# Two chained attention layers on one core: the second layer's denominators by 32x32 transposes and one product, a third buffer for its high parts, and projections one step later

## The chip, the core and the metric

The kernel runs on one core of a Trainium2 chip. The metric is the device time of one execution in microseconds, lower is better. Three executions of the kernel before are given by their median, and one more execution was profiled.

The engines have these names throughout: PE multiplies matrices (PEld is its weight load), DVE is the vector engine, ACT the scalar engine that computes exponentials, POOL the general one that here also issues many transfers, and SP only issues transfers. SBUF is the working memory of 128 partitions, and PSUM holds the results of PE.

## The reference

The input x has 4 images of 64x64 pixels with 256 channels, so 4 images of 4096 tokens. Two attention layers follow each other, each over all the tokens of one image, with queries and keys of 32 channels. The second layer has values of 128 channels and a projection back to 256.

```python
# layer 0
q, k, v = x @ Wq + bq, x @ Wk + bk, x @ Wv + bv          # 32, 32, 256 channels
attn = softmax(einsum('bnd,bmd->bnm', q, k))
x = gamma * einsum('bnm,bmc->bnc', attn, v) + x
# layer 1
f, g, v = x @ Wf + bf, x @ Wg + bg, x @ Wh + bh          # 32, 32, 128 channels
beta = softmax(einsum('bqd,bkd->bqk', g, f))
out = x + (beta @ v) @ Wo + bo
```

All arrays are in float32.

## The kernel before

`fast_path` does all the work. It computes exp of the scores without first taking off a maximum, and at its end counts on DVE and PE whether denominators, values and gamma stayed in a safe span; the count goes to a flag, and `general_path`, a slower way, would run only if the flag were above zero.

**Blocks and steps.** For each image b and layer l the queries are cut into blocks j, and the keys of a block into steps i. In the first layer (l = 0) there are 16 blocks of 256 queries, with 8 steps of 512 keys. In the second layer (l = 1) there are 8 blocks of 512 queries, with 16 steps of 256 keys. A `Step` computes the scores on PE into PSUM (`st`, L532), ACT takes exp of them into an SBUF tile `p` of 128x1024 (L544), and PE multiplies with the values and accumulates over the steps of the block (L582 in the first layer, L600 in the second).

**Parts.** A full float32 product is slow on PE, so the first layer, and six of the sixteen steps of the second (`SPLIT1`: 0, 3, 5, 8, 11, 13), are computed in parts in the faster format float32r: ACT computes exp twice, once rounded into `high` (L542) and once into `p`; DVE makes `low` = p - high (L555) and `d` from both (L560); PE makes one product from each of the three. The ten other steps of the second layer use p as a whole, in float32.

**Denominators.** In the first layer a column of ones beside the values gives the sum of the weights with the product. In the second layer it is summed apart. The p tiles of the steps in `MOVED_SUMS` (0, 4, 7, 9, 12) are summed by transfers: POOL issues a copy of the first into the tile `p_sum_moved` (L548) and adds each of the others to it with an accumulating transfer (L550). The p tiles of the eleven other steps are added by DVE into the tile `p_sum` (L571, L573). At the end of a block `end_second` adds both (L659) and folds the two halves into `sums`, 128x512 (L660). The sum over the 128 partitions is then made by PE for each 128 queries: `sums` is the loaded side and one column of ones is multiplied with it (L668), beside the output projection (L667) into the same PSUM tile. DVE takes the reciprocal (L670), ACT scales with it (L673), and POOL issues the accumulating transfer to the output (L675). There are four such outputs to a block, and `plan` puts them at steps 1 to 4 of the next block, so that those of an image's last block fall into the first layer of the next image.

**The next projections.** `project_units` makes queries, keys and values of half a block of 256 tokens in three units: a transpose of loaded squares on DVE (L392) with a split into parts, the queries and keys (L422, L439 to L446), and the values (L464). In the second layer, `plan` places those of the next image with `i = 12 + 7 * h - j * NI[1]`, h from 0 to 15: a transpose there, the queries and keys two steps later, the values three steps later. The last image has none.

**Buffers.** `wide` gives out the tiles of 128x1024. Tag "t" has two buffers, for `high` of both layers and for p of split steps in the second layer; "p" has three; "d" and "e" have one each. "d" serves `d` in the first layer and `p_sum` in the second, and "e" is for `p_sum_moved`. Tag "small" has four buffers of 128x256: for the residual rows x_res, the rows x1 of the first layer's result, and the outputs y. The projected queries and keys `qk` (L439, L440) have a buffer of their own. PSUM results beside scores and products share two buffers, `side_psum`.

**What sets the order.** The loop at the end of `fast_path` runs the steps one after the other and calls `scores()` two steps ahead. The program goes through a scheduler that keeps dependencies, allots the buffers and orders each engine's instructions by its own estimate; each engine then runs its instructions strictly in that order. An instruction that waits stops all that stands behind it on its engine.

Of the kernel before, what the change touches and what calls it, by code (L numbers as in the profile page):

```python
# [57 lines left out]
P = 128  # L58
# [10 lines left out]
MOVED_SUMS = (0, 4, 7, 9, 12)  # L69
# [169 lines left out]
def fast_path(ctx: ExitStack, tc: tile.TileContext, x, w0, w1, wo, bo, gamma, out, off):  # L239
# [27 lines left out]
    def wide(tag, name, dtype=F32):  # L267
        return work.tile([P, 2 * QB], dtype, tag=tag, bufs={"d": 1, "e": 1, "p": 3}.get(tag, 2), name=name)
# [41 lines left out]

    inverse = const.tile([P, 2, B * N // P], F32, name="inverse")
# [12 lines left out]
    for l, (q_w, q_b, k_w, k_b, v_w, v_b) in enumerate((w0, w1)):  # L324
        queue = (nc.scalar, nc.gpsimd)[l]
        w_sb = work.tile([P, NCC, 2 * D], F32, tag="small", bufs=4, name=f"wqk_whole{l}")
        b_sb = const.tile([2 * D, 1], F32, name=f"bqk{l}")
        for g, w_dram, b_dram in ((0, q_w, q_b), (D, k_w, k_b)):
            queue.dma_start(w_sb[:, :, g : g + D], w_dram.rearrange("(c p) d -> p c d", p=P))
            queue.dma_start(b_sb[g : g + D, :], b_dram.rearrange("(d o) -> d o", o=1))  # L330
        w_parts = const.tile([P, NCC, 4 * D], F32R, name=f"wqk{l}")
        high, low = w_parts[:, :, : 2 * D], w_parts[:, :, 2 * D :]
        nc.scalar.copy(high, w_sb)
        nc.vector.tensor_sub(low, w_sb, high.bitcast(F32))
        wqk.append(w_parts)
        bqk.append(b_sb)
        v_sb = const.tile([P, NCC, CV[l]], F32, name=f"wv{l}")
        queue.dma_start(v_sb, v_w.rearrange("(c p) d -> p c d", p=P))
        wv.append(v_sb)
# [20 lines left out]
    def bias_units():  # L360


        def issue():
            nc.vector.tensor_scalar(bv, bv, gamma_sb, None, ALU.mult)
            wide_bias = work.tile([P, P], F32, tag="small", bufs=4, name="wide_bias")
# [10 lines left out]
    q_t, moved_sums, first_p, waiting = {}, {}, [], {}  # L376
# [35 lines left out]
    def project_units(b, l, h):  # L412
# [5 lines left out]
        def qk_unit():  # L418
# [10 lines left out]
            whole = data.tile([2 * D, QB0], F32, tag="qk", name=f"qk_{b}_{l}_{h}")  # L429
# [61 lines left out]
    def load_rows(dst, parts, which, order):  # L491
        for n, h in enumerate(order):
            nc.gpsimd.dma_start(dst[n * D : (n + 1) * D, :], parts[h, which])
# [16 lines left out]
    def small(name):  # L510
        return work.tile([P, C], F32, tag="small", bufs=4, name=name)


    class Step:
# [8 lines left out]
        def scores(self):  # L523
# [16 lines left out]
            if self.split:  # L540
                self.high = wide("t", f"high_{self.key}", F32R)
                nc.scalar.activation(self.high, s_flat, AF.Exp, bias=down)  # L542
            self.p = wide("t" if self.split and l == 1 else "p", f"p_{self.key}")
            nc.scalar.activation(self.p, s_flat, AF.Exp)  # L544
            if l == 1 and i in MOVED_SUMS:
                if i == MOVED_SUMS[0]:
                    moved_sums[b, j] = wide("e", f"p_sum_moved_{b}_{j}")
                    nc.gpsimd.dma_start(moved_sums[b, j], self.p)  # L548
                else:
# [14 lines left out]
        def add_up(self, p_sum):  # L564
# [5 lines left out]
            elif self.i == kept[1]:  # L570
                nc.vector.tensor_add(p_sum, first_p.pop(0), self.p)  # L571
            else:
                nc.vector.tensor_add(p_sum, p_sum, self.p)  # L573
# [80 lines left out]
    def end_second(b, j, acc, p_sum, o):  # L654
        key = f"{b}_{j}"
        for h in range(QB // QB0):
            nc.vector.tensor_add(o[h][:, :QB0], o[h][:, :QB0], acc[1][:, h * QB0 : (h + 1) * QB0])
        sums = work.tile([P, QB], F32, tag="sums", bufs=1, name=f"sums_{key}")
        nc.vector.tensor_add(p_sum, p_sum, moved_sums[b, j])  # L659
        nc.vector.tensor_add(sums, p_sum[:, :QB], p_sum[:, QB:])  # L660

        def output(t):
            def issue():
# [4 lines left out]
                nc.tensor.matmul(ps[:, C : C + 1], sums[:, tok], ones[:, :1], start=True, stop=True)  # L668
                n = (b * N + j * QB) // P + t
                nc.vector.reciprocal(inverse[:, 1, n : n + 1], ps[:, C : C + 1])  # L670
# [8 lines left out]
        return [output(t) for t in range(NT)]  # L679

    def run(units):
        for u in units:
            u()

# [15 lines left out]
    acc, p_sum, units = None, None, {}  # L700

    def plan(b, l, j, ends):
# [20 lines left out]
        else:  # L723
            for n, u in enumerate(ends):
                put(1 + n, u)
        if b + 1 < B:
            for h in range(NH):
                i = 12 + 7 * h - j * NI[1]
# [6 lines left out]
    for n, s in enumerate(steps):  # L735
        b, l, j = s.b, s.l, s.j
        if s.first:
# [5 lines left out]
            if l == 1:  # L743
                p_sum = wide("d", f"p_sum_{b}_{j}")
# [24 lines left out]
        s.add_up(p_sum)  # L769
# [31 lines left out]
        if s.last:  # L801
            ends = end_first(b, j, acc) if l == 0 else end_second(b, j, acc, p_sum, o)
    run(ends)

    good = small("good").rearrange("p (l n) -> p l n", l=2)
    nc.vector.tensor_scalar(good, inverse, 1.0 / SUM_MAX, None, ALU.is_ge)
    nc.vector.tensor_scalar(inverse, inverse, 1.0 / SUM_MIN, None, ALU.is_le)
    nc.vector.tensor_mul(good, good, inverse)  # L810
    nc.vector.tensor_scalar(seen_v, seen_v, VALUE_MAX, None, ALU.is_le)
    size = const.tile([P, 1], F32, name="size")
    nc.vector.tensor_mul(size, gamma_sb, gamma_sb)
    nc.vector.tensor_scalar(size, size, GAMMA_MAX**2, None, ALU.is_le)
    low = const.tile([P, 1], F32, name="low")
    for seen, axes in ((good, AX.XY), (seen_v, AX.XY)):
        nc.vector.tensor_reduce(low, seen, axes, ALU.min)
        nc.vector.tensor_mul(size, size, low)
# [54 lines left out]
```

## Time and profile before

| what | value |
|---|---|
| median of three executions | 3158.18 us (3157.30 to 3159.27) |
| the profiled execution: own time | 3155.92 us |
| the profiled execution: span from first to last instruction | 3154.1 us, 1.8 us less |
| PE, PEld busy | 3116.3 us (99%), 2672.0 us (85%) |
| DVE busy | 2689.1 us (85%) |
| ACT busy | 2140.1 us (68%) |
| POOL busy | 900.7 us (29%) |
| transfers | 239.49 MB, mean 76 GB/s |
| granted clock of PE, mean | 0.998 |

A row of a group in the profile names line, engine and operation, output and inputs, shapes and count; behind the first bar stand busy time and mean duration of one, behind the second how long the engine had been idle just before, and for whom. A row of the timeline has its start in us, its length, the engine, and how many equal instructions follow each other. Matmuls overlap, so their modelled lengths are longer than the distance between their starts; what one costs is read from the starts. A float32 matmul appears as two records, a float32r one as one.

### The profile page before, as it was taken

How to read it: one execution, taken by the hardware profiler on the slowest of the kernel's cores; microseconds unless marked ns; L12 is line 12 of the kernel's file. 1: busy time of each engine (PE TensorE's matmuls, PEld its weight loads, DVE VectorE, ACT ScalarE, POOL GpSimd, SP SyncE). 2: the span in 40 equal slices, each digit the busy share in tenths (PEclk: the TensorE clock that was granted, in tenths of full speed). 3: DMA queues.
4: the chain of work that ended last, by engine and by line, in shares of the span. 5: the costliest groups of instructions: out<-in, count | busy, mean ns of one | idle time of the engine just before them, and what ended most of it. 6: DMA issues, size and time to landing. Idle time of an engine off the chain costs nothing.

```text
span 3154.1 us, 54090 instructions
## 1 busy us (share of the span) xinstructions
PE 3116.3 (99%) x19908; PEld 2672.0 (85%) x19908; DVE 2689.1 (85%) x3237; ACT 2140.1 (68%) x2835; POOL 900.7 (29%) x1108
## 2 busy tenths in 40 slices
PE   8999999999999999999999999999999999999997
PEld 7999998666799999866679999976668999996664
DVE  7888888888888888888888888898888888888876
ACT  7666666777666666777766666677776666666674
POOL 5232224222422222422242222232223222233221
PEclk9999999999999999999999999999999999999999
DMA  4121114555512121555541112255554111125454
GB/s 119 43 53 47 48 48 104 107 108 105 104 44 51 41 53 47 113 101 112 107 93 47 49 45 51 51 116 107 105 113 81 48 46 47 49 65 105 97 95 73
DMA packets 391392, 239.49 MB, mean 76 GB/s; under 512 B 266672, under 2 KB 355248, under 8 KB 391120
## 3 DMA queue, kind: packets, MB, share of 16 engines
q0 software_dynamic: 68160, 134.86, 22.0%
q1 hardware_dynamic: 322048, 100.76, 13.4%
q8 instruction: 161, 2.64, 0.4%
q14 instruction: 111, 0.91, 0.1%
q10 hardware_dynamic: 912, 0.33, 0.1%
HBM read 82.58 MB, written 67.11 MB: 47 GB/s over the span
## 4 chain that ended last, share of the span: by engine, by line
PE 91%; DVE 3%; DMA 2%; issue 2%; ACT 1%; POOL 0%; SPq 0%; DVEq 0%; ACTq 0%; POOLq 0%
PE acc L600 24%; PE acc L582 23%; PE acc_pair L582 23%; PE st L532 14%; PE psv L464 4%; PE psqk L422 2%; PE pso L667 2%; DVE d L560 1%; DVE low L555 1%; ACT p L544 1%; DVE p_sum L573 1%; DMA p_sum_moved<-p 0%; DMA squares<-in_x 0%; PE pso L668 0%; DMA squares<-x_dram 0%
## 5 line engine op out<-in xcount | busy, mean ns | idle before, releaser
L542 ACT ACTIVATE high<-st,down 128x1024 fp32r<-128x1024 f32 x704 | 786.5, 1117 | 703.2 <-PE st L532 362.8
L544 ACT ACTIVATE p<-st 128x1024 f32<-128x1024 f32 x1024 | 1042.5, 1021 | 166.3 <-PE st L532 143.8
L560 DVE SCALAR_TENSOR_TENSOR d<-low,high 128x1024 fp32r<-128x1024 f32 x704 | 871.0, 1237 | 227.0 <-PE acc_pair L582 223.7
L555 DVE TENSOR_TENSOR low<-p,high 128x1024 fp32r<-128x1024 f32 x704 | 936.6, 1330 | 142.6 <-ACT p L544 141.6
L532 PE MATMUL st<-q,k 128*128 128x256 f32 (+1 forms) x3072 | 706.3, 338 | 2.5 <-DMA k<-qk_parts 1.4
L600 PE MATMUL acc<-p,v 128*128 128x512 f32 x1280 | 611.0, 597 | 0.0
L532 PEld LDWEIGHTS st<-q,k 128*128 128x128 f32 x3072 | 470.0, 189 | 103.3 <-issue 40.6
L639 POOL TENSOR_TENSOR x_res<-x,bo 128x256 f32<-128x256 f32 x128 | 212.5, 1660 | 879.3 <-DVE x L628 879.2
L600 PEld LDWEIGHTS acc<-p,v 128*128 128x128 f32 x1280 | 233.1, 189 | 161.8 <-issue 143.4
L573 DVE TENSOR_TENSOR p_sum<-p_sum,p 128x1024 f32<-128x1024 f32 x288 | 352.6, 1224 | 9.4 <-ACT p L544 5.8
L582 PE MATMUL acc<-v0h,high 128*128 128x258 f32 x2048 | 341.6, 284 | 1.2 <-ACT high L542 1.2
L582 PE MATMUL acc<-v0d,d 128*128 128x258 f32 x2048 | 339.2, 287 | 2.6 <-DVE d L560 2.2
L582 PE MATMUL acc<-v0l,low 128*128 128x256 f32 (+1 forms) x2048 | 329.3, 283 | 0.6 <-DVE low L555 0.5
L582 PE MATMUL acc_pair<-v0h,high 128*128 128x258 f32 x2048 | 329.8, 283 | 0.0
L582 PE MATMUL acc_pair<-v0l,low 128*128 128x256 f32 (+1 forms) x2048 | 328.8, 282 | 0.0
L582 PE MATMUL acc_pair<-v0d,d 128*128 128x258 f32 x2048 | 328.5, 282 | 0.0
L582 PEld LDWEIGHTS acc<-v0h,high 128*128 128x128 f32 x2048 | 286.0, 189 | 3.1 <-issue 1.4
L582 PEld LDWEIGHTS acc<-v0d,d 128*128 128x128 f32 x2048 | 281.5, 190 | 5.6 <-DVE d L560 4.9
L582 PEld LDWEIGHTS acc<-v0l,low 128*128 128x128 f32 x2048 | 282.2, 190 | 1.8 <-DVE low L555 1.3
L582 PEld LDWEIGHTS acc_pair<-v0h,high 128*128 128x128 f32 x2048 | 282.1, 189 | 0.0
L582 PEld LDWEIGHTS acc_pair<-v0l,low 128*128 128x128 f32 x2048 | 281.1, 189 | 0.0
L582 PEld LDWEIGHTS acc_pair<-v0d,d 128*128 128x128 f32 x2048 | 281.0, 189 | 0.0
(108 smaller groups left out, 3332.5 us busy)
## 6 DMA issues: line engine op xcount, KB each, us to landing
p_sum_moved<-p POOLq DMA_DIRECT2D x160, 512.0 KB, 4.7
x_res<-in_x SPq DMA_DIRECT2D x128, 128.0 KB, 2.1
qk_dram<-qk_parts SPq DMA_DIRECT2D x128, 128.0 KB, 1.9
x_dram<-x SPq DMA_DIRECT2D x128, 128.0 KB, 1.7
out<-x_res SPq DMA_DIRECT2D x128, 128.0 KB, 1.7
squares<-x_dram SPq DMA_DIRECT2D x512, 32.0 KB, 1.9
out<-y POOLq DMA_DIRECT2D x128, 128.0 KB, 3.2
q<-qk_dram POOLq DMA_DIRECT2D x252, 64.0 KB, 2.2
```

Source lines behind the costliest of these rows:

```text
L422: nc.tensor.matmul(ps, wqk[l][:, c, :], x_parts[key][n][:, c, :], start=(c == n == 0), stop=(c == NCC - 1 and n == 1),)
L464: nc.tensor.matmul(ps[:, t, :], xT[key][:, c, t * P : (t + 1) * P], wv[l][:, c, :], start=(c == 0), stop=(c == NCC - 1),)
L532: nc.tensor.matmul(st[:, g, :], k_t[b, l, kt // NT][:, kt % NT * P : (kt % NT + 1) * P], q_t[b, l, j * n // QB][:, q0 : q0 + n], start=Tru ...
L542: nc.scalar.activation(self.high, s_flat, AF.Exp, bias=down)
L544: nc.scalar.activation(self.p, s_flat, AF.Exp)
L555: nc.vector.tensor_sub(self.low, self.p, self.high.bitcast(F32))
L560: nc.vector.scalar_tensor_tensor(self.d, self.low.bitcast(F32), -UP, self.high.bitcast(F32), ALU.mult, ALU.add)
L573: nc.vector.tensor_add(p_sum, p_sum, self.p)
L582: nc.tensor.matmul(acc[2 * s + which][:, :width], p[:, g * QB0 + s * P : g * QB0 + (s + 1) * P], v0[self.i][v][:, g, :width], start=self.f ...
L600: nc.tensor.matmul(acc[which], v_part[:, g, :], p[:, g * QB : (g + 1) * QB], start=first and g == 0, stop=last and g == G[1] - 1,)
L639: nc.gpsimd.tensor_add(x_old[s], x_new[s], bo_sb)
L667: nc.tensor.matmul(ps[:, :C], part, wo_sb, start=True, stop=True)
```

## The change

1. **Denominators.** The moved sum is added into `p_sum` first, and the fold stays inside that tile. A new unit `turn` transposes the folded 128x512 in squares of 32x32 into the other half of the same tile and sums each 32 elements into `part_sums`, 128x16. A new unit `denominators` makes one product with the matrix `same` (ones where two rows have the same number modulo 32), which gives a 128x16 tile of PSUM, and takes four reciprocals of 32x4 from it. The four products with ones and four reciprocals of 128x1 go. The units stand at steps 1 and 2 of the next block, and the four outputs at steps 3 to 6. The very last block keeps the old way. POOL builds `same` once at the start, with seven instructions.
2. **Who sums.** `MOVED_SUMS` has six steps in place of five, beginning with step 3. The p of step 3 is written straight into the tile of tag "e", so the first copy goes, and five accumulating transfers remain. Ten steps are left to DVE. `p_sum` is allotted at its first addition. The accumulating transfers are ordered behind the transfers issued before them on POOL.
3. **Buffers.** A tag "t_more" with one buffer takes every third tile of `high` and split p in the second layer. "small" has three buffers in place of four, and `qk` now comes from it too. `sums` has no tile of its own any more.
4. **Projections.** 12 becomes 13.
5. **The check.** All but the last four columns of denominators are checked during the last block, with a tile from "t", and the end checks four columns.

The core of the diff ("..." stands for what is left out):

```diff
-MOVED_SUMS = (0, 4, 7, 9, 12)
+MOVED_SUMS = (3, 4, 6, 7, 9, 12)
...
-        return work.tile([P, 2 * QB], dtype, tag=tag, bufs={"d": 1, "e": 1, "p": 3}.get(tag, 2), name=name)
+        return work.tile([P, 2 * QB], dtype, tag=tag, bufs={"d": 1, "e": 1, "p": 3, "t_more": 1}.get(tag, 2), name=name)
...
+    same = const.tile([P, P], F32, name="same")
+    nc.gpsimd.tensor_copy(same[:, :S], ident[:, :S])
+    for a in range(1, P // S):
+        nc.gpsimd.tensor_add(same[:, :S], same[:, :S], ident[:, a * S : (a + 1) * S])
+    for a in range(1, P // S):
+        nc.gpsimd.tensor_copy(same[:, a * S : (a + 1) * S], same[:, :S])
...
-            whole = data.tile([2 * D, QB0], F32, tag="qk", name=f"qk_{b}_{l}_{h}")
+            whole = small(f"qk_{b}_{l}_{h}")[: 2 * D, :]
...
     def small(name):
-        return work.tile([P, C], F32, tag="small", bufs=4, name=name)
+        return work.tile([P, C], F32, tag="small", bufs=3, name=name)
+    def turn_of_t():
+        turns[0] += 1
+        return "t_more" if turns[0] % 3 == 0 else "t"
...
-                self.high = wide("t", f"high_{self.key}", F32R)
+                self.high = wide(turn_of_t() if l == 1 else "t", f"high_{self.key}", F32R)
                 nc.scalar.activation(self.high, s_flat, AF.Exp, bias=down)
-            self.p = wide("t" if self.split and l == 1 else "p", f"p_{self.key}")
+            base = l == 1 and i == MOVED_SUMS[0]
+            self.p = wide("e" if base else turn_of_t() if self.split and l == 1 else "p", f"p_{self.key}")
             nc.scalar.activation(self.p, s_flat, AF.Exp)
-            if l == 1 and i in MOVED_SUMS:
-                if i == MOVED_SUMS[0]:
-                    moved_sums[b, j] = wide("e", f"p_sum_moved_{b}_{j}")
-                    nc.gpsimd.dma_start(moved_sums[b, j], self.p)
-                else:
+            if base:
+                moved_sums[b, j] = self.p
+            elif l == 1 and i in MOVED_SUMS:
+                with tc.issue_after(loads[0].ins):
                     nc.gpsimd.dma_start(moved_sums[b, j], self.p, accum_op=ALU.add)
...
+        def turn():
+            nc.vector.transpose(squares, sums)
+            nc.vector.tensor_reduce(part_sums, squares.rearrange("p (n k) -> p n k", k=S), AX.X, ALU.add)
+        def denominators():
+            ps = side_psum(f"psd_{key}")[:, : QB // S]
+            nc.tensor.matmul(ps, same, part_sums, start=True, stop=True)
+            for a in range(P // S):
+                rows = slice(a * S, (a + 1) * S)
+                of_rows = ps[rows, :].rearrange("p (t a) -> p t a", a=P // S)[:, :, a]
+                nc.vector.reciprocal(inverse[rows, 1, n0 : n0 + NT], of_rows)
...
                 nc.tensor.matmul(ps[:, :C], part, wo_sb, start=True, stop=True)
-                nc.tensor.matmul(ps[:, C : C + 1], sums[:, tok], ones[:, :1], start=True, stop=True)
-                n = (b * N + j * QB) // P + t
-                nc.vector.reciprocal(inverse[:, 1, n : n + 1], ps[:, C : C + 1])
+                n = n0 + t
+                if end:
+                    nc.tensor.matmul(ps[:, C : C + 1], sums[:, tok], ones[:, :1], start=True, stop=True)
+                    nc.vector.reciprocal(inverse[:, 1, n : n + 1], ps[:, C : C + 1])
...
-        return [output(t) for t in range(NT)]
+        return ([] if end else [turn, denominators]) + [output(t) for t in range(NT)]
...
-                i = 12 + 7 * h - j * NI[1]
+                i = 13 + 7 * h - j * NI[1]
```

## The prediction

> **What bounds the kernel now.** I read the page's busy line and chain first, then PE's timeline in both layers, then the groups and the waits.
>
> ```profile
> PE 3116.3 (99%) x19908; PEld 2672.0 (85%) x19908; DVE 2689.1 (85%) x3237; ACT 2140.1 (68%) x2835; POOL 900.7 (29%) x1108
> PE 91%; DVE 3%; DMA 2%; issue 2%; ACT 1%; POOL 0%; SPq 0%; DVEq 0%; ACTq 0%; POOLq 0%
> ```
>
> Nine tenths of the chain that ended last are PE. Busy PE can hide slack, so I take distances between starts from the timeline of PE, first in a block of the second layer (last image, no projections beside it):
>
> ```profile
> 2957.67 0.63 PE L600 MATMUL acc<-high,v 128*128 128x512 f32 x2
> ...
> 2959.05 0.59 PE L667 MATMUL pso<-wo,o 128*128 128x256 f32 x2
> 2959.49 0.28 PE L668 MATMUL pso<-ones,sums 128*128 128x1 f32 x2
> 2959.62 1.96 PE L600 MATMUL acc<-p,v 128*128 128x512 f32 x4
> 2961.02 1.04 PE L600 MATMUL acc<-d,v 128*128 128x512 f32 x2
> ...
> 2971.89 1.88 PE L600 MATMUL acc<-p,v 128*128 128x512 f32 x4
> 2973.21 1.03 PE L600 MATMUL acc<-d,v 128*128 128x512 f32 x2
> ```
>
> The same `high` of the next block starts at 2993.18, so a block takes 35.51 us. Its work: 32 score products and 36 products in parts at 0.23 us (2957.67 to 2958.14 is two) make 15.6; ten whole steps of four records at 0.43 make 17.2; four output projections at 0.43 make 1.7; the four products with ones 0.9 (below). The sum is 35.4, which leaves 0.1 us idle: PE is saturated. Blocks beside projections take 40 us and are within some 1 us of a like sum. In the first layer a steady block takes 28.2 us (1042.97 from 1014.75, with starts 0.12 apart throughout): saturated too. There DVE is busy 24.5 of 28.2 us, and in the second layer it is this (the windows view: us, PE, PEld, DVE, ACT, POOL, clock, DMA share and GB/s; first with projections, then without):
>
> ```profile
> 601.20:641.20 40.00, 40.00 (x149) 26.64 (x148) 34.59 (x43) 29.38 (x41) 9.40 (x13) 1.00 0.56 106
> 2922.10:2957.60 35.50, 35.50 (x125) 22.74 (x125) 28.36 (x31) 24.35 (x28) 9.59 (x13) 1.00 0.52 97
> ```
>
> DVE has 5 to 7 us to spare in a block, ACT over 10, POOL 26. So what leaves PE shortens the kernel; what moves between DVE, ACT, POOL and transfers costs only where PE then waits.
>
> [...] POOL's L550 waited 45.2 us in all for `p_sum_moved`.
>
> **The change part by part.** The groups that give prices, with mean ns behind the first bar:
>
> ```profile
> L573 DVE TENSOR_TENSOR p_sum<-p_sum,p 128x1024 f32<-128x1024 f32 x288 | 352.6, 1224 | 9.4 <-ACT p L544 5.8
> L392 DVE STREAM_TRANSPOSE xT<-squares 128x512 f32<-128x512 f32 x112 | 79.0, 705 | 15.2 <-DMA squares<-in_x 6.5 <-DMA squares<-x_dram 5.1 <-issue 3.0
> L668 PE MATMUL pso<-ones,sums 128*128 128x1 f32 x256 | 36.2, 211 | 0.2
> L670 DVE RECIPROCAL inverse<-pso 128x1 f32<-128x1 f32 x128 | 20.5, 162 | 15.2 <-PE pso L668 14.2
> L817 DVE TENSOR_REDUCE low<-good 128x1 f32<-128x256 f32 x1 | 0.4, 420 | 0.0
> L817 DVE TENSOR_REDUCE low<-seen_v 128x1 f32<-128x128 f32 x1 | 0.3, 286 | 0.0
> ```
>
> *PE.* A product with ones is two records. They start 0.13 us before what follows (2959.49 to 2959.62), and the whole step behind them then takes 1.40 us to the next start, against 1.32 without them (2971.89 to 2973.21): 0.22 us each, 0.88 a block. The one product with `same` has as many records and loads as large a side; 16 columns in place of one: 0.2 to 0.3, I take 0.22. Net 0.66 us a block, in 31 of 32 blocks: **-20.5 us**, all of it on the path.
>
> *DVE.* Off: one addition, 1.22. On: a transpose as L392, 0.71, and a reduction of 128x512. The two rows of L817 differ by 134 ns for 128 elements, so 0.69 for 512 ([...] at least 0.42). Reciprocals: four of about 0.16 before and after. Net +0.2 us a block, under 5 to 7 us of idle; without that cover 31 x 0.2 = 6. But the 1.4 us stand at the block's start, ahead of the next `low` and p_sum. The fold ends 1.0 to 2.6 us after the block's first product in most blocks, so the 16 sums are ready at 2.4 to 4 us, 0.7 later where a projection's transpose comes between; the product stands after about 4.9 us of PE's work (four score products and four in parts for 1.84, a whole step 1.72, a `d` 0.46, half a whole step 0.86). Mostly covered; late in one or two blocks an image, where the fold came 2.7 and 3.7 us after the start. What is late next is `low` of step 3, needed at 7.3 us. I put 0.8 us an image for three images: **+2.5** (0 to 8).
>
> *Edge between second and first layer.* `p_sum` and the first layer's `d` share one buffer. `d` of step 0 now waits for turn and reduction, 1.4 us on DVE, and the product stands on PE ahead of the `d` products. Before, `d` ended at 848.87 and PE took it at 849.14: nothing covers it. Three edges at 1.2: **+3.5** (0 to 4.5).
>
> *Buffers.* A third "t" lets ACT begin `high` of step 13 before PE is done with `high` of step 11. PE's blocks beside projections have 2 to 4 us an image above my sum, 9 us in all: **-2** (0 to -9). "small" with three: in the first layer x1 of the second half takes the slot of x1 of the first, so DVE waits for the store and for POOL's addition. Both ended about 1048.6, DVE came at 1049.59: 1 us of cover, cost 0; without it 1 us for each of 64 blocks, partly under DVE's 3.7 us idle. Loads of x_res move on SP behind the eight of squares (they end about 1064.9, the rows are then in SBUF with POOL's bias by 1070, wanted at 1074.5): 0. y and qk wait for an output's transfer of three steps, 7 us, earlier, which lands in 3.2: 0.
>
> *Transfers and queues.* One copy issue (0.56 us on POOL) goes, one accumulating issue (0.88) comes; five stay. Each waits for the one before, 4.7 us from issue to landing; exps of 4, 6, 7, 9, 12 are 2.5 us a step apart, so only 7 and 9 wait, about 4 and 2 us, and the last lands some 9 us before the fold. Outputs queue behind them and are not awaited for 7 us. No cost; without slack, ACT would wait for buffer "p".
>
> *Projections one step on* move DVE, ACT, PE and SP's eight loads together by 2.5 us within an idle-free PE: 0 (-1 to 1).
>
> *Start and end.* Seven small POOL operations (0.1 to 0.3 each, as its memset of 0.20) delay gamma's load, for which DVE waited 0.67 us at 12.81 us: **+0.8** (0 to 2). At the end:
>
> ```profile
> 3140.65 0.29 DVE L808 TENSOR_SCALAR good<-inverse 128x256 f32<-128x256 f32 x1 [1.99 <-DMA out<-y]
> ...
> 3143.53 0.15 DVE L822 CAST off<-count 1x1 int32<-1x1 f32 x1 [0.37 <-PE count L821]
> ```
>
> The check waited 1.99 us for a "small" buffer under an output's transfer, then ran 2.9 us. With four columns and another buffer the flag is there about 3 us sooner, but the last output still lands at 3143.4: **-2.5** (0 to -3.2).
>
> **Sum.** -20.5 + 2.5 + 3.5 - 2 + 0.8 - 2.5 = -18.2 against the profiled execution's own 3155.9 us: 3137.7. The median stands 2.3 above that one: **3140.0**. A measurement of this kernel tells about 0.2%, 6.3 us, from no change.
>
> **The rivals.**
>
> 1. *PE loses the products and most arrives* (the sum): 0.62, own range 3132 to 3150.
> 2. *The third buffer also frees the second layer.* For it: in the waits view ACT's `high` waited 110.3 us for acc_pair and 20.3 for d. Against: PE's idle there is 9 us altogether, so no more can come. 3140.0 - 7 - 3.5 (edges free) = 3129.5: 0.16.
> 3. *Slower: PE meets `same` before DVE has the sums.* PE's order is strict; the product stands in the block's third step, and everything behind it, whole steps too, waits. It decides from 0.66 us a block, where it eats the saving. With transpose and reduction wholly on the path, 1.4 us in 31 blocks, it is 31 x (1.4 - 0.66) = +23, so 3140 + 20.5 + 23 - 2.5 = 3181. For it: PE did wait for the fold at L668, 16 times, 6.5 us. Against: the product now stands 2 us later than that one did, and DVE has idle time. 0.12.
> 4. *It doesn't do what it says*: weight loads of ones were hidden, [...] and PE gains 5 us, eaten by the edges. Against: 35.4 + 0.1 accounts for the block only with 0.22. 3158: 0.10.
>
> **The numbers.** Cases 1 and 2 are faster by over 0.2%, and a fifth of 4: 0.80. Same: the rest of 4, 0.08. Slower: 0.12. The range leaves out case 3, some of 4 and the far end of 2: 3126 to 3158.
>
> **What would show it.** In the changed profile: L668's rows only 8, the new product 62 records; blocks of the last image 34.85 us apart; first-layer blocks still 28.2; the edges' first block about 29 to 30 us against 30.07; PE waiting for part_sums under 8 us in all; DVE's busy share up by 0.2%. I am wrong if last-image blocks stay above 35.3, if PE waits for part_sums over 0.5 us in most blocks, if first-layer blocks grow (DVE's x1 waiting for POOL or a store), or if ACT waits for the accumulating transfers.

## The result and the profile after

The changed kernel is **slower**: 3237.52 us median (3233.11 to 3238.87, four executions) against 3157.74 us for the kernel before beside it, a ratio of 1.0251 (95% interval 1.0233 to 1.0268), or +79 us. The prediction was 3140 us, with a range to 3158.

The busy line of the page and the chain by engine, after:

```profile
PE 3140.3 (97%) x19722; PEld 2666.5 (82%) x19722; DVE 2715.1 (84%) x3272; ACT 2135.6 (66%) x2835; POOL 895.9 (28%) x1115
PE 68%; DVE 10%; issue 8%; DMA 6%; SPq 2%; ACT 1%; POOL 1%; DVEq 0%; POOLq 0%; ACTq 0%
```

PE has 186 records fewer, as meant, and yet 24 us more busy time, in a span 83 us longer. Of the chain that ended last PE now has only two thirds: DVE, issues and transfers have moved in. The groups that answer to those shown of before (busy and mean behind the first bar, idle before and for whom behind the second):

```profile
L591 DVE TENSOR_TENSOR p_sum<-p_sum,p 128x1024 f32<-128x1024 f32 x256 | 312.2, 1220 | 24.8 <-ACT p L561 22.3
L687 DVE TENSOR_REDUCE part_sums<-p_sum 128x16 f32<-128x512 f32 x31 | 20.8, 670 | 0.5
L692 PE MATMUL psd<-part_sums,same 128*128 128x16 f32 x62 | 10.2, 240 | 1.5 <-DVE part_sums L687 1.3
L706 PE MATMUL pso<-ones,p_sum 128*128 128x1 f32 x8 | 1.1, 228 | 0.0
L600 PE MATMUL acc<-v0d,d 128*128 128x258 f32 x2048 | 348.7, 291 | 27.7 <-DVE d L577 26.6
```

The new denominators are there and cheap: a reduction of 0.67 us (0.69 was estimated), 62 records of the product, eight of the old ones, and PE's matrix products waited 1.3 us for `part_sums`. The last row is the surprise. It is a product of the **first** layer, which the change was not meant to touch: it waited 26.6 us for `d`, against 2.2 us for the same row before:

```profile
L582 PE MATMUL acc<-v0d,d 128*128 128x258 f32 x2048 | 339.2, 287 | 2.6 <-DVE d L560 2.2
```

The row of its weight loads waited 42.7 us for `d`, against 4.9 before.

I read block lengths as in the prediction, from one block's first product to the next one's. Means in us of the profiled executions; the steady first-layer block is the median of blocks 3 to 14, and j counts the second layer's blocks of an image from 0:

| kernel | first-layer block, steady | j = 0 | j = 5, first three images | last image, j = 2 to 6 | j = 1 to 7 together, first three images | ratio to before |
|---|---|---|---|---|---|---|
| before | 28.21 | 38.5 | 40.2 | 35.51 | 283.1 | 1 |
| after | 28.89 | 45.0 | 45.7 | 35.13 | 286.8 | 1.0251 |

So the loss sits in three places: +0.7 us in nearly all 64 first-layer blocks (44 us), +6.5 us in each image's first second-layer block (26 us), +5.4 us in the sixth block of three images (16 us). That is 86 us; other second-layer blocks gave some of it back. Where nothing else happens (last image), the block is 0.38 us shorter, as hoped in sign.

**Place one, the first layer.** The timeline of the changed kernel where two half blocks meet:

```profile
981.99 3.47 POOL L813 TENSOR_TENSOR x_res<-x_res,bv 128x256 f32<-128x256 f32 x2 [3.12 <-DMA squares<-x_dram]
...
983.09 1.77 DVE L572 TENSOR_TENSOR low<-p,high 128x1024 fp32r<-128x1024 f32 x1
...
985.12 0.90 DVE L414 TENSOR_TENSOR xl<-xT,xh 128x512 fp32r<-128x512 f32 x1
...
985.93 1.21 DVE L577 SCALAR_TENSOR_TENSOR d<-low,high 128x1024 fp32r<-128x1024 f32 x1
...
987.20 0.75 PE L600 MATMUL acc<-v0d,d 128*128 128x258 f32 x4 [0.31 <-DVE d L577]
```

POOL's two additions of the bias to x_res run exactly while DVE makes `low` and `xl` of the boundary. `low` takes 1.77 us there and 1.22 where no addition of POOL runs beside it, `xl` 0.90 for 0.68; `d` behind them comes late, and PE waits for it. At other boundaries `d` itself is the one that takes 1.7 us for 1.22. In the kernel before these additions ran in mid-block, here 8.8 us after the block's first product at 1042.97:

```profile
1051.12 1.76 DVE L555 TENSOR_TENSOR low<-p,high 128x1024 fp32r<-128x1024 f32 x1
1051.76 1.73 POOL L751 TENSOR_TENSOR x_res<-x_res,bv 128x256 f32<-128x256 f32 x1
...
1053.20 1.37 DVE L560 SCALAR_TENSOR_TENSOR d<-low,high 128x1024 fp32r<-128x1024 f32 x1 [0.32 <-PE acc_pair L582]
```

`low` is just as slow there, but DVE is ahead: `d` behind it waits for PE, and not PE for `d`. With four small buffers one was free early, and SP's load and POOL's addition went ahead. Now `qk` and x_res come from three buffers, and SP issues the loads only behind the eight of squares.

**Place two, the sixth block** (same view, second image):

```profile
1551.65 0.87 POOL L567 DMA_DIRECT2D p<-p  x1 [4.22 <-issue]
1552.20 2.98 POOL L712 DMA_DIRECT2D out<-y  x3
...
1557.76 0.37 ACT L447 COPY qk<-psqk 64x256 f32<-64x256 f32 x1 [4.65 <-DMA out<-y]
...
1558.69 0.79 PE L472 MATMUL psv<-wv,xT 128*128 128x256 f32 x1 [3.50 <-DVE qk L448]
```

`qk` waits for the buffer of a `y` whose output is still under way; the output was issued by POOL behind an accumulating transfer. ACT stands still for 4.65 us, and PE for 3.5.

**Place three, the first block**, shows in the windows view (us, then PE, PEld, DVE, ACT, POOL busy, granted clock, DMA share, GB/s; second image, then a whole block of the last image):

```profile
1364.40:1367.00 2.60, 0.48 (x2) 0.04 (x1) 2.58 (x3) 0.66 (x2) 2.20 (x4) 1.00 0.43 101
1367.00:1373.80 6.80, 6.12 (x17) 5.03 (x17) 2.40 (x3) 2.93 (x4) 1.18 (x3) 0.50 0.56 101
3077.06:3112.20 35.14, 35.10 (x119) 21.96 (x118) 28.91 (x32) 24.12 (x28) 9.92 (x13) 1.00 0.56 98
```

PE is all but idle for 2.6 us, since xh of the next image's first half block comes late; and then its **clock is granted at half** for 6.8 us. The trace has eight such stretches of 3.4 or 6.8 us in the changed kernel between 90 us and the tail, 41 us together, seven of them beginning in an idle gap of PE of over 2 us or within 1.4 us behind one; the kernel before has none there. The mean clock fell from 0.998 to 0.992, and 0.006 x 3237 is 19 us: by this estimate about a quarter of the loss is not waiting but slow running in and after waits.

### The profile page after: what moved, and what is told of

Its sections match the earlier page's. It is cut to its first block, busy times and chain, and to the rows that moved or that the text cites. A ratio compares the mean times of both kernels' runs of the same rounds, so it can differ in the third digit from the quotient of the medians.

```text
span 3237.0 us, 53894 instructions
## 1 busy us (share of the span) xinstructions
PE 3140.3 (97%) x19722; PEld 2666.5 (82%) x19722; DVE 2715.1 (84%) x3272; ACT 2135.6 (66%) x2835; POOL 895.9 (28%) x1115
## 4 chain that ended last, share of the span: by engine, by line
PE 68%; DVE 10%; issue 8%; DMA 6%; SPq 2%; ACT 1%; POOL 1%; DVEq 0%; POOLq 0%; ACTq 0%
PE acc L618 19%; PE acc_pair L600 17%; PE acc L600 15%; PE st L547 11%; DVE d L577 4%; PE psv L472 3%; DVE low L572 3%; DMA p<-p 2%; PE psqk L430 1%; DMA x_res<-in_x 1%; DMA out<-y 1%; SPq L280 1%; PE pso L703 1%; DVE xl L414 1%; DMA squares<-x_dram 1%
## 5 line engine op out<-in xcount | busy, mean ns | idle before, releaser
L572 DVE TENSOR_TENSOR low<-p,high 128x1024 fp32r<-128x1024 f32 x704 | 947.7, 1346 | 116.8 <-ACT p L561 116.5
L600 PE MATMUL acc<-v0d,d 128*128 128x258 f32 x2048 | 348.7, 291 | 27.7 <-DVE d L577 26.6
L567 POOL DMA_DIRECT2D p<-p x160 | 142.5, 891 | 695.7 <-ACT p L561 297.0
L591 DVE TENSOR_TENSOR p_sum<-p_sum,p 128x1024 f32<-128x1024 f32 x256 | 312.2, 1220 | 24.8 <-ACT p L561 22.3
L600 PEld LDWEIGHTS acc<-v0d,d 128*128 128x128 f32 x2048 | 282.1, 190 | 46.9 <-DVE d L577 42.7
L657 POOL TENSOR_TENSOR x_res<-x,bo 128x256 f32<-128x256 f32 x128 | 203.8, 1592 | 406.0 <-DVE x L646 406.0
L813 POOL TENSOR_TENSOR x_res<-x_res,bv 128x256 f32<-128x256 f32 x128 | 159.0, 1259 | 496.1 <-DMA x_res<-in_x 246.5
L600 PEld LDWEIGHTS acc<-v0l,low 128*128 128x128 f32 x2048 | 282.0, 190 | 0.9 <-DVE low L572 0.8
```

The source lines that it names most:

```text
L567: nc.gpsimd.dma_start(moved_sums[b, j], self.p, accum_op=ALU.add)
L572: nc.vector.tensor_sub(self.low, self.p, self.high.bitcast(F32))
L591: nc.vector.tensor_add(p_sums[self.b, self.j], so_far, self.p)
L600: nc.tensor.matmul(acc[2 * s + which][:, :width], p[:, g * QB0 + s * P : g * QB0 + (s + 1) * P], v0[self.i][v][:, g, :width], start=self.f ...
L657: nc.gpsimd.tensor_add(x_old[s], x_new[s], bo_sb)
L813: nc.gpsimd.tensor_add(x_res[b, j][t], x_res[b, j][t], bv)
```

## The experiments

All ratios are to the kernel before, measured beside it on the same chip, with 95% intervals; a thousandth is 3.2 us. Line numbers move a little between kernels. The block lengths of all of them stand in a table at the end of this section.

### The ring of small buffers

**e1_rings**: four small buffers, `qk` by itself, no third buffer for high parts.

```diff
-tag="small", bufs=3
+tag="small", bufs=4
-whole = small(f"qk_{b}_{l}_{h}")[: 2 * D, :]
+whole = data.tile([2 * D, QB0], F32, tag="qk", ...)
-return "t_more" if turns[0] % 3 == 0 else "t"
+return "t"
```

> The changed kernel with its buffers given back: four small buffers, qk in a buffer of its own, and to make room no third buffer for high parts. Turn, one product for the denominators and the later start of projections stay. Theory R (the shared ring of three small buffers holds qk, x_res and y back): the additions of x_res return to mid-block, first-layer blocks go from 28.9 back to 28.2 us (-50), the second layer's first and sixth blocks lose their long gaps (-30), so 3140 to 3160 us, below the kernel before. Rival D (turn, reduction and the one product make DVE late): 3215 to 3237, blocks of the first layer stay at 28.9. Rival S (projections one step on make the gaps of the second layer): about 3190, the first layer cured, the second not.

Measured 3176.37 us, ratio 1.0059 (1.0043 to 1.0076). The first layer is cured (28.21), the sixth block too (40.0), the first block not (43.2). Ring and third buffer together are three quarters of the loss, as theory R has it, but 19 us remain that it did not foresee.

**e2_own_qk**: the same, with three small buffers.

> The same, but the small ring stays at three buffers and only qk has its own buffer again (no third buffer for high parts). It parts the ring's two edits. If qk in the ring is the whole cause: as the first kernel, 3140 to 3160 us. If three buffers alone make the additions of x_res late in the first layer and qk the gaps of the second: first layer still 28.9 us a block, second layer cured, about 3195 us. Rival D: 3215 to 3237.

Measured 3183.73 us, 1.0081 (1.0064 to 1.0098). So `qk` in the ring was nearly all of it; the fourth buffer adds some 7 us, with intervals that overlap. My split (three buffers hurt the first layer, `qk` the second) was wrong: the first layer is 28.3 with three.

**e3_before_rings**: the kernel before with the ring alone (three small buffers, `qk` among them).

> The kernel before with one part of the change alone: three small buffers, qk among them. Denominators by four products with ones, projections at their old step, two buffers for high parts. Theory R: it takes most of the loss, first-layer blocks 28.9 us and gaps at qk in the second layer, 3158 + 50 to 85 = 3208 to 3243 us. Rival D and rival S: 3158 to 3165.

Measured 3218.29 us, 1.0189 (1.0172 to 1.0206): +60 us, with first-layer blocks of 28.88 and a first block of 43.4. The ring alone makes most of the loss, from the other side, and it makes the first block long although the moved sums are the old ones. The sixth block stays at 40.5: there the ring alone is not enough.

**e8_no_bias**: the changed kernel without POOL's additions of the value bias to x_res, which is then missing from the result. Its other additions, of `bo` (L657), stay.

```diff
 nc.sync.dma_start(x_res[b, j][t], x[b, row : row + P, :])
-nc.gpsimd.tensor_add(x_res[b, j][t], x_res[b, j][t], bv)
```

> The changed kernel with its rings, leaving out POOL's additions of the first layer's value bias to x_res (two of 128x256 a half block, 128 in all); the loads of x_res stay where the ring put them. Theory C (these additions, now at the block's boundary, run beside DVE's low and d and make d late): first-layer blocks go from 28.9 to 28.2 us, 3237 - 45 = 3192 us; the second layer is not helped. Rival: DVE waits there for a ring buffer or a load itself, and blocks stay at 28.9 us, 3237.

Measured 3192.46 us, 1.0117 (1.0102 to 1.0133), 42 us less than the changed kernel by the ratios. Its groups:

```profile
L572 DVE TENSOR_TENSOR low<-p,high 128x1024 fp32r<-128x1024 f32 x704 | 919.1, 1306 | 118.8 <-ACT p L561 118.4
L600 PE MATMUL acc<-v0d,d 128*128 128x258 f32 x2048 | 339.9, 287 | 6.0 <-DVE d L577 5.9
```

First-layer blocks are 28.21 again, PE's wait for `d` falls from 26.6 to 5.9 us, and the mean of `low` from 1346 to 1306 ns, while loads, ring and DVE's order stay. The second layer is not helped (45.7 in the sixth block). So it was neither the ring nor the load that stopped DVE: the ring **moved** 128 cheap additions to where they cost. `low` and `xl` read two tiles each, and the trace shows both longer beside POOL's addition (1.77 us for 1.22, 0.90 for 0.68); by what mechanism, no run here shows.

### Projections, moved sums, third buffer

**e4_twelve**: the changed kernel with 12 for 13.

> The changed kernel with the projections at their old step (12 for 13), nothing else. Rival S: the gaps ahead of psqk in the second layer's first blocks (2.8 us and the half clock after them) go, 3237 - 15 to 30 = 3207 to 3222 us. Theory R: the ring's waits stay, 3230 to 3240 us.

Measured 3222.92 us, 1.0201 (1.0184 to 1.0218): the gain of about 16 us is there, but the first block stays at 44.9, and the gaps ahead of psqk stay too (PE idle for 2.8 us in both kernels). It is the sixth block that loses its stall (40.0); a shorter one, PE idle for 2.0 to 3.4 us ahead of psv, appears in the second block instead (43.0 for 39.8), where the projection now comes beside the outputs. Right number, wrong place.

**e12_no_third_t**: the changed kernel with its third buffer for high parts taken away.

> The changed kernel with its third buffer for high parts taken away, all else as it is. Theory T: last-image blocks 35.1 to 35.3-35.4 us and the other second-layer blocks 0.3 longer, 3237 + 5 to 10 = 3242 to 3247 us. Rival (the third buffer is without effect): 3235 to 3240 us.

Measured 3227.73 us, 1.0226 (1.0212 to 1.0240): 8 us **faster** by the ratios, whose intervals just overlap, against both theories. Last-image blocks do grow (35.13 to 35.25), but the sixth blocks fall from 45.7 to 40.0: with the third buffer the meeting of `qk` and an output was worse than without.

**e6_rings_twelve** and **e7_rings_moved** start from e1_rings; the first takes 12, the second the old set of moved sums.

```diff
-MOVED_SUMS = (3, 4, 6, 7, 9, 12)
+MOVED_SUMS = (0, 4, 7, 9, 12)
...
-self.p = wide("e" if base else turn_of_t() if ...
+self.p = wide(turn_of_t() if ...
...
-moved_sums[b, j] = self.p
+moved_sums[b, j] = wide("e", ...)
+nc.gpsimd.dma_start(moved_sums[b, j], self.p)
...
-with tc.issue_after(loads[0].ins):
```

> The kernel of e1_rings (four small buffers, qk by itself, no third buffer for high parts) with the projections at their old step as well. What then stays of the change is the denominators, the new set of moved sums and the early check. Theory M (the second layer's first block is long because steps 0 to 2 are now added on DVE, beside the end of the first layer): it still takes 43 us, 3165 to 3176 us. Theory S (it is the start of projections): first blocks back to 39 us, 3150 us.

> The kernel of e1_rings with the old set of moved sums instead (0, 4, 7, 9, 12, copied to its buffer by a transfer and not forced behind the loads); projections one step on stay. Theory M: the second layer's first block returns from 43.2 to 39 us in all four images, so 3176 - 16 = 3160 us or a little below. Theory S: the first block stays at 43 us, 3170 to 3176 us.

Measured 3172.05 us, 1.0045 (1.0031 to 1.0058), and 3166.59 us, 1.0032 (1.0020 to 1.0045). The first block is 43.9 with 12 and 38.8 with the old set: theory M. (With the ring as in e3 it is long even so; each of the two suffices, and what of the ring does it was not tried.) The timeline of e1_rings shows how, at the start of the last image's second layer:

```profile
2868.06 1.22 DVE L591 TENSOR_TENSOR p_sum<-p,p 128x1024 f32<-128x1024 f32 x1
...
2869.38 1.23 DVE L591 TENSOR_TENSOR p_sum<-p_sum,p 128x1024 f32<-128x1024 f32 x1
...
2872.09 0.87 DVE L646 SCALAR_TENSOR_TENSOR x<-o,g,x_res 128x256 f32<-128x256 f32 x2
```

With step 0 no longer moved, DVE adds in steps 1 and 2, and both additions stand ahead of the first layer's last rows `x`, which come 7.0 us after their first `o`; in e7 it is 3.4 us. e7 also gives back the copy and the old order of issues, which were not tried apart from the set. Everything for the last half block of keys hangs on those rows: store, squares, transpose, `qk`, load of k. At 2900.07 PE waits 2.29 us for that k. What e7 keeps of the change beside the denominators is the later start of projections and the early check, and its blocks j = 1 to 7 take 285.1 us an image, against 281.2 in e5, which has neither.

### The denominators by themselves

**e5_denominators**: the kernel before with transpose, reduction and one product, and nothing else.

> The kernel before with the denominators alone: transpose, reduction and one product in 31 blocks, sums in place; old ring, old start of projections, old set of moved sums, check at the end as before. Theory P (the prediction's PE term holds, and what ate it are the other parts): -20.5 of PE, +2.5 and +3.5 for DVE and edges, so 3143 us (3138 to 3150), last-image blocks 34.85 us, PE waiting for part_sums under 8 us. Rival D (DVE late at the block's start): 3158 or more.

Measured 3154.69 us, 0.9998 (0.9990 to 1.0007): **no change**. The other parts did not eat 20 us; they were never there. Last-image blocks are 35.44, not 34.85.

**e16_no_ones**: the kernel before, without the products with ones, and nothing in their place. Each reciprocal reads a column of `sums` itself, so the denominators are wrong, and DVE no longer waits for PE there.

> The kernel before, leaving out the 128 products with ones (each reciprocal takes a column of sums itself, so the denominators are not those of the reference); nothing takes their place. It is the ceiling of what any cheaper denominator can bring. Theory of the prediction (PE is saturated and all that leaves it counts): 4 x 0.22 a block, 32 blocks: 3156 - 28 = 3128 us, last-image blocks 34.63. Rival A (ACT and DVE follow 0.1 us behind PE, and hold st back next): 3140 to 3150 us, last-image blocks 35.0 to 35.4.

Measured 3134.21 us, 0.9921 (0.9907 to 0.9935): 25 us, of 28 expected. The timeline of two blocks of the last image:

```profile
2975.64 0.63 PE L600 MATMUL acc<-high,v 128*128 128x512 f32 x2
...
3010.27 0.63 PE L600 MATMUL acc<-high,v 128*128 128x512 f32 x2
```

34.63 us, exactly 35.51 less four times 0.22 (the mean of 34.85 in the table holds one block of 35.73). So PE was the bound and a product with ones did cost 0.22; rival A falls for these blocks. The prices of what was taken away were right. With the one product at 0.22 as well, blocks of e5 should be 34.85; they are 0.6 longer.

**e13_later_product**: e5 with the product one step later.

```diff
-return ([] if end else [turn, denominators]) + [output(t) for t in range(NT)]
+def both():
+    denominators()
+    output(0)()
+return [output(t) for t in range(NT)] if end else [turn, lambda: None, both] + [output(t) for t in range(1, NT)]
```

> The kernel of e5_denominators with the product (and its four reciprocals) one step later, ahead of the first output; the outputs stay at their steps. Theory L (PE meets the product some 0.2 us before DVE has part_sums in most blocks, and up to 0.9 at the edges between layers): PE's waits for part_sums vanish, last-image blocks 35.43 to 35.2, edges' first block 31.05 to 30.2 us, 3155 - 6 to 8 = 3147 to 3149 us. Rival A (PE is held by ACT's exp and DVE's d anyway, which the wait only hid): 3153 to 3157 us.

Measured 3159.05 us, 1.0000 (0.9992 to 1.0008). Last-image blocks are 34.98, better than expected and 0.46 less than in e5. The timeline of e5 shows what the early place costs, in a block whose first product starts at 2991.24:

```profile
2994.81 0.63 PE L539 MATMUL st<-q,k 128*128 128x512 f32 x2
...
2995.47 0.30 PEld L680 LDWEIGHTS psd<-part_sums,same 128*128 128x128 f32 x2 [0.46 <-DVE part_sums L675]
2995.47 0.39 PE L680 MATMUL psd<-part_sums,same 128*128 128x16 f32 x2
...
2995.71 1.96 PE L607 MATMUL acc<-p,v 128*128 128x512 f32 x4
...
3002.91 0.30 PEld L539 LDWEIGHTS st<-q,k 128*128 128x128 f32 x2 [0.32 <-ACT p L551]
...
3004.17 0.30 PEld L607 LDWEIGHTS acc<-low,v 128*128 128x128 f32 x2 [0.25 <-DVE low L562]
```

Two score products take 0.46 us where nothing waits (2992.17 to 2992.63), here 0.66: PE meets the product 0.20 us before the sums. The next product then starts 0.24 us behind it, 0.14 in the 22 blocks of e5 where the sums are in time. So the early place costs 0.30 us here. The product itself costs 0.22, as expected (0.14, and 0.08 by which the step behind takes longer; 0.23 in e13). The last 0.29 over e16's 34.63 stand later in the block, where loads wait for `p` of ACT and `low` of DVE; in e13 0.12 of that are left.

By PE's starts the product comes too early in six blocks of the last image (0.20 us each) and at the three edges (PE idle for 0.6 us each), some 3 us in all. The group of its weight loads says more:

```profile
L680 PEld LDWEIGHTS psd<-part_sums,same 128*128 128x128 f32 x62 | 10.5, 188 | 14.7 <-DVE part_sums L675 12.0 <-issue 2.4
```

12.0 us stand there, where the matrix product's own row shows 1.8. But 0.24 us stands ahead of such a load also where the sums are in time (in the first image's sixth block they were ready 0.5 us before the product), so neither row is the cost. And the time of the whole did not follow: the sixth blocks grew from 40.3 to 41.4, and j = 1 to 7 of the other images took 282.0 us for 281.2.

**e9_third_t**, **e10_later_fold**, **e11_both** look for room in another way: e5 with a third buffer (`qk` then lies in PSUM and in `qk_parts`, and small has three), e5 with the fold one step later, and both.

> The kernel of e5_denominators with the third buffer for high parts of the second layer. Room for it: qk is held in PSUM and in qk_parts, without a buffer of its own, and the small ring has three buffers (without qk). Theory T (in e5 the 0.66 us that PE lost a block came back as ACT's high waiting for a t buffer that DVE's d holds at the block's start; a third buffer lets ACT go on): last-image blocks 35.43 to 34.9-35.1 us, 3155 - 10 = 3145 us, up to 7 more for three small buffers (e2 against e1), so 3142 to 3152. Rival W (what remains is PE's own: the one product and outputs apart from each other cost what the four products did): blocks stay at 35.4 us, 3155 to 3162.

> The kernel of e5_denominators with the fold of the moved sums and of the two halves (1.22 and 0.69 us of DVE) put one step later, together with the transpose, in all blocks but an image's last. Theory T: DVE's d of step 0 comes 1.9 us sooner, ACT's high is released sooner, last-image blocks 35.43 to 35.0-35.2 us, 3155 - 5 to 10 = 3145 to 3150. Rival: the lateness only moves from d of step 0 to the sums and low of the next split step (PE waits for part_sums), 3155 to 3165.

> Third buffer as in e9_third_t and later fold as in e10_later_fold together. Theory T: last-image blocks 34.85 us, 3138 to 3148 us. Rival W: 3155.

Measured 1.0039 (1.0025 to 1.0053), 1.0011 (1.0005 to 1.0018) and 1.0049 (1.0036 to 1.0063). Theory T holds for the last image in e9 (35.09, with the product as early as in e5: the waits later in the block are gone) and for j = 1 to 7 of the others (279.3 for 281.2 an image), but the first block takes 42.0 for 38.8; whether three small buffers or `qk` in PSUM does that was not tried apart. The later fold brings nothing (35.56).

**e14_edge** and **e15_later_edge**: e5 with sums and their transpose in other buffers at the edges between layers; the second with e13's later product as well.

```diff
+if j == NQ[1] - 1 and b < B - 1:
+    sums = work.tile([P, QB], F32, tag="sums", bufs=1, ...)
+    nc.vector.tensor_add(sums, p_sum[:, :QB], squares)
+    squares = work.tile([P, QB], F32, tag="squares", bufs=2, ...)
```

> The kernel of e5_denominators with sums and their transpose in two other buffers at the three edges from second to first layer (one of its own, one of the ring of squares), so that the first layer's d does not wait for transpose and reduction. If the shared buffer is the edges' cost: the edges' first block 31.05 to 30.1-30.5 us and its second 27.5 to 27.2, 3155 - 3 = 3152 us. If the product with same, ahead of the d products on PE, is the cost: no change, 3155.

> e13_later_product and e14_edge together. Theory L: edges' first block 30.1 us, last-image blocks 35.2, 3145 to 3148 us, which is under both kernels. Rival A: 3152 to 3155.

Measured 0.9994 (0.9986 to 1.0003) and 0.9987 (0.9980 to 0.9994). The edge's first block falls from 31.05 to 30.25: 0.8 of the 1.0 us that e5 had added was the shared buffer.

**e17_chosen**: e15 with the earlier product in blocks j = 4 and 5 of the first three images, and the changed kernel's early check.

> The kernel of e15_later_edge (product one step later, sums at the edges in other buffers) with the product at the earlier step again in the fifth and sixth second-layer block of the first three images, where e13 and e15 were 0.2 to 1.1 us longer than e5, and with the changed kernel's check of all but the last block ahead of the end. Expected: sixth blocks 41.3 to 40.2 us, 3 x 1.3 = -4, the end -2.5, from a ratio of 0.9987 to one of 0.9965 to 0.9975, 3148 to 3151 us at a before of 3158.6. Rival: the sixth block's length comes from where the outputs stand and not from the product, and only the end is gained: 0.998.

Measured 3148.94 us against 3157.02, **0.9977 (0.9967 to 0.9987)**: 7 us faster than before and 86 faster than the changed kernel. The sixth blocks gained less than expected (41.6 to 40.7); the last block fell from 55.6 to 53.9, for the flag comes sooner after the last products. The flag's gain is partly e15's own loss, for the last block of the kernel before took 54.4. The page of e17 reads like that of the kernel before:

```profile
PE 3104.0 (99%) x19722; PEld 2649.0 (84%) x19722; DVE 2733.8 (87%) x3304; ACT 2133.6 (68%) x2835; POOL 902.9 (29%) x1115
PE 90%; DVE 3%; DMA 2%; issue 2%; ACT 2%; POOL 1%; SPq 0%; DVEq 0%; ACTq 0%; POOLq 0%
```

| kernel | first-layer block, steady | j = 0 | j = 5, first three images | last image, j = 2 to 6 | j = 1 to 7 together, first three images | ratio |
|---|---|---|---|---|---|---|
| e1_rings | 28.21 | 43.2 | 40.0 | 35.27 | 281.8 | 1.0059 |
| e2_own_qk | 28.31 | 44.7 | 39.9 | 35.28 | 282.3 | 1.0081 |
| e3_before_rings | 28.88 | 43.4 | 40.5 | 35.51 | 283.2 | 1.0189 |
| e4_twelve | 28.91 | 44.9 | 40.0 | 35.13 | 282.4 | 1.0201 |
| e5_denominators | 28.21 | 38.8 | 40.3 | 35.44 | 281.2 | 0.9998 |
| e6_rings_twelve | 28.32 | 43.9 | 40.7 | 35.26 | 280.4 | 1.0045 |
| e7_rings_moved | 28.21 | 38.8 | 40.0 | 35.43 | 285.1 | 1.0032 |
| e8_no_bias | 28.21 | 44.6 | 45.7 | 35.13 | 286.4 | 1.0117 |
| e9_third_t | 28.28 | 42.0 | 39.9 | 35.09 | 279.3 | 1.0039 |
| e10_later_fold | 28.21 | 38.8 | 40.5 | 35.56 | 282.4 | 1.0011 |
| e11_both | 28.27 | 42.6 | 40.2 | 35.21 | 279.5 | 1.0049 |
| e12_no_third_t | 28.88 | 44.9 | 40.0 | 35.25 | 283.3 | 1.0226 |
| e13_later_product | 28.21 | 38.8 | 41.4 | 34.98 | 282.0 | 1.0000 |
| e14_edge | 28.21 | 38.8 | 40.5 | 35.43 | 281.4 | 0.9994 |
| e15_later_edge | 28.31 | 38.9 | 41.6 | 34.97 | 281.7 | 0.9987 |
| e16_no_ones | 28.31 | 39.2 | 39.4 | 34.85 | 277.0 | 0.9921 |
| e17_chosen | 28.21 | 38.8 | 40.7 | 34.98 | 280.9 | 0.9977 |

## Why the prediction was wrong

The +79 us come off in this order, by the ratios: third buffer 8 (e12), `qk` out of the ring 45 (e2), fourth small buffer 7 (e1), then projections at 12 alone 4 (e6) or the old moved sums alone 9 (e7), and with both, and without the early check and the late allotting of `p_sum`, 19 (e5). The last 6 of those 19 were not taken apart. Each ratio has an interval of about 5 us to either side, so the steps under 10 us are rough.

- **"Loads of x_res move on SP behind the eight of squares (...): 0."** This is the step that failed, and the dearest. I asked only whether the rows would be there in time, and they were (DVE waited 1.5 us for them in the whole changed kernel). I did not ask what POOL's addition, moved along, would run beside. The sign that I had named, growing first-layer blocks, was the one that came, though not by x1's wait. In the trace of before `low` was already longer beside POOL's additions in mid-block (1.76 us), where nothing waited for it; at the boundary PE does. Price 0; measured about 42 us (e8).
- **"y and qk wait for an output's transfer of three steps, 7 us, earlier, which lands in 3.2: 0."** The order by which `qk` meets a `y` shifts from block to block (a half block every seven steps, a block every sixteen), and in the sixth it met one that had just been issued. Outputs also land later: 5.0 us in the middle by the page for 3.2 (5.0 in e1 too, 3.5 in e5, which has the old set of moved sums). 5.4 us in each of three blocks, with half a clock behind some (0.50 for 3.4 us from 1558.2).
- **The moved sums.** I priced POOL's issues and transfers and found no cost, which was so. I never asked which of DVE's additions change places: two now stand ahead of the rows that the last keys hang on. 9 us alone (e7, with the copy and the order of issues).
- **Projections one step on, 0 (-1 to 1).** 4 us alone (e6), and 16 in company with the ring (e4). I looked at them inside PE, where they are indeed free; what moved is the blocks in which they meet the outputs.
- **The third t buffer, -2 (0 to -9).** In the range where nothing else was in the way: -1.9 us in each of three images over j = 1 to 7 in e9, and 0.35 a block in the last. In the changed kernel +8.
- **The PE term of -20.5.** Both prices are confirmed: 0.22 for a product with ones (e16), 0.22 to 0.23 for the one with `same` (e5, e13). So 0.66 a block did leave PE. What failed is that all of it would be on the path: of 0.66 in a block of the last image 0.07 arrived (e5), and of 4.6 us in blocks 1 to 7 of another image 1.9.
- **Turn and reduction late at the block's start, +2.5 (0 to 8).** At the product itself the size was right: some 3 us in e5. The working was not. PE stands at the product after 4.04 us, not 4.9, in a block without projections, for the half step that I had put ahead of it comes behind; and the sums are ready after 4.17, not 2.4 to 4. It is rival 3's place, at less than its price. I had no term for what follows: ACT's `p` and DVE's `low` later in the block, 0.29 in each such block. The sign that I named, PE waiting for part_sums under 8 us, could not show that; and of its two rows in the changed kernel, 1.3 at the product and 10.0 at the loads, neither is the cost.
- **The edges, +3.5.** Right in mechanism (e14) and a little small: first and second block of the first layer together +1.4 us in e5, three times.
- **The end, -2.5.** Not to be seen in the changed kernel (its last block is 54.5 for 54.4, with everything behind it late). In e17 the last block is 1.7 us shorter than in e15, but only 0.5 shorter than in the kernel before.

What held: the bound. PE was saturated, and my sum of 35.4 us for a block was good enough that taking 0.88 away gave 34.63. What did not follow is that on a PE with 0.1 us of slack **every other engine's move is a risk**, and I had priced all of those at or near nothing.

Still open: why blocks beside projections keep so little, though by PE's starts the product comes in time there. In e13 j = 1 to 7 are 5.1 us an image longer than in e16, 0.7 a block, where the product explains 0.23.

## What to carry to other kernels

Where one engine has no slack left, price an edit of the buffers by what it **moves**: list every instruction that a later buffer delays, and look which instructions of other engines it then runs beside, not only whether it meets its deadline. A ring shared by tiles of different periods meets its worst case somewhere; look for the block in which they collide. And price the new work with the same care as the old: a saving is worth little if the thing that replaces it is asked for a fifth of a microsecond too early and the engines behind it come late in turn.

## What the runs showed of the hardware

- **DVE slowed beside POOL's addition.** `low` (128x1024, two tiles read) took 1.77 us for 1.22, `xl` 0.90 for 0.68, and `low` did so in the kernel before too (1.76 us).
- **PE ran at half clock in and after gaps of 2.2 to 4.9 us, though not every time.** In the changed kernel seven of eight stretches of 3.4 or 6.8 us at clock 0.50 began in such an idle gap of PE or up to 1.4 us behind it (idle for 2.8 us until 1367.7, at 0.50 from 1367.0); the eighth, at 90.4, had none over 1.2 us near it. Behind another gap, idle for 2.8 us until 569.8, the clock stayed at 1.00. What decides it, no run here shows.
- **An instruction that waited held up what stood behind it on its engine.** In the changed kernel ACT was idle for 4.65 us ahead of `qk` at 1557.76. The scores that the `high` behind it reads were made by 1553.90, and it started at 1558.15, after `qk`.
- **A float32 product took PE longer than a float32r one.** For 128x512 in the block of before from 2957.67, by PE's starts: two records of 0.43 us each with p, one of 0.23 with a part.
- **A wait can stand with the weight load, and overstate.** When both sides of a small product are late, look at the row of its PEld as well (12.0 us there, 1.8 at the product, in e5), and then at the starts of PE's products, which lost some 3 us.
